# Fused attention stage of a two-layer decoder: opening reordered, output projection by quarters, convolution one frame ahead

## The chip, the cores and the metric

The kernel runs on one core of one Trainium2 chip. The metric is the device time of one launch in microseconds (us). One execution was profiled as well; every duration of a single instruction below comes from that one execution.

The engines are named as in the profile: PE is TensorE's matmul side and PEld its weight loads, DVE is VectorE, ACT is ScalarE, POOL is GpSimd, SP is SyncE, which only issues DMAs. Each of them works through a queue of its own in order, and they meet through semaphores.

## The reference

A decoder of two layers works on x (4 sequences, called frames here, of 512 positions and 256 channels) and a context of 4 x 512 x 192. The change concerns the first two of its six sublayers, which the kernel fuses into one stage. Cut to what matters:

```python
def _L0_attn_ref(x, ...):            # x is the layer-normed input; 16 heads of 32
    xc = causal_conv_4_taps(x, conv_w) + conv_b
    qk = einsum('btc,ec->bte', xc, qk_w).reshape(B, T, 16, 32)
    q = k = qk / max(norm(qk), 1e-12)
    v = einsum('btc,ec->bte', xc, v_w)
    g = sigmoid(einsum('btc,ec->bte', xc, g_w) + g_b)
    angles = t * freqs
    state = (v * cos(angles) + v * shift_by_one(k)) * g
    decay = gamma ** t
    mem = cumsum(state * decay, axis=1) / (decay + 1e-06)
    out = einsum('bte,ce->btc', mem * q, o_w)
    return layernorm(out) * ln_g + ln_b

x = x + _L0_attn_ref(layernorm(x), ...)
x = x + cross_attention(layernorm(x), ctx, Wq, bq, Wk, bk, Wv, bv, Wo, bo)   # 16 heads of 16, 512 x 512 softmax
```

The other four sublayers (a mixture of experts, and a second layer) come after the stage and are not touched.

## The kernel before, in words

`l0_mixers` holds the stage, one Python function with many small helpers, and has three parts. An **opening** loads weights and computes what the first frame needs before its first score. A **loop of 16 units** then runs the cross attention: a unit is four heads of one frame, so four units make a frame. A unit has eight score tiles of 128 x 1024 (`exponents`, L908 to L919): PE writes the scores into one of two PSUM pairs, DVE takes the row maxima (`tops`, L916), ACT takes the exponentials (`e`, L919); the sums over values follow a unit later (`gather_values`, L948). A short **tail** closes the last frame.

The first sublayer of a later frame runs inside the units of earlier ones. In the unit loop `after(n, f, ...)` puts a step f behind the n-th score tile of the unit, n from 0 to 7, its slot. With b the frame of the unit and m its number in the frame, `near_b` is b + 1 and `next_b` is b + 2. The steps of a frame are, in order:

- `normalize` (L725) normalizes x (DVE) and adds ln_b to x on POOL. `mix` (L739 to L750) turns a half of the channels on PE, copies it twice on ACT and does three taps of the convolution on DVE; there are two mixes for a frame.
- `measure` (L752) makes qk on PE for four heads' worth of channels and squares it on ACT; `total` (L767) sums the squares on PE; `scale`, `scale_near`, `scale_far` and `factor` (L772 to L797) send the sums through DRAM, take the inverse root on DVE (the rn chain), multiply by the decays, and spread the two factors over the channels by DMA.
- `gated_values` (L799) makes g and v, `recall` (L809 to L823) the running memory: a product with the factor on DVE, an add of cos on POOL, a product, a scan and two products on DVE. It ends in qk times memory (L823), in place.
- `emit` (L825 to L829) is the output projection: 32 passes on PE for a frame, four groups of channels summed into each of four row blocks, which fill two PSUM banks. It runs by halves: `emit(b, 0)` and `emit(b, 2)` each need all four groups, thus all four recalls. `absorb` (L831 to L840) is the layernorm of the result (its statistics are `ln_st` L179, in a helper) and the addition to x. `tokens`, `turn_tokens`, `split` and `keep` then make the queries of the cross attention.
- `keys` and `keep_keys` (L1018, L1023) make keys and values of a frame from the context, with a high and a low half of the keys (`low_k` is DVE's, L855), and put them in DRAM. All four frames' keys are made in the opening.

Only in the opening: `decays` (L675 to L692) doubles the powers of gamma in ten steps on DVE and stores them (`far_dec`); `cosines` (L703 to L719) needs `time`, an iota on POOL (L705), six DVE operations for each of four channel groups to reduce the angle, sine and square on ACT, and two operations on POOL, the last of which multiplies by a decay that `decay_of` (L698) loads by DMA. `fetch_bias` (L619 to L626) brings the key and query biases in eight loads each of 16 x 2 elements, in an order of its own, and v_bias comes in four loads; `dense` (L628) packs and scales weights and biases on POOL.

Two things set the order. Matmuls (`pinned`, L577) and loads on SP (`move`, L586) keep the order of the program; where one of them waits, what stands behind it on its engine waits too. All else is put in order ahead of time by the framework's scheduler, by its own estimates; each engine then executes its queue as it stands. Buffers are rotating pools: `bank` is four PSUM banks for all that isn't a score, `scratch` eight tiles of 128 x 516, `wide` (tag `e`) eleven tiles of 128 x 1024, `factors` two. The order of the opening is written out in L1034 to L1108, the slots in L1109 to L1187.

Of the kernel before, what the change touches and what calls it, by code (L numbers as in the profile page):

```python
# [19 lines left out]
NB = 4  # L20
# [520 lines left out]
def l0_mixers(k):  # L541
# [20 lines left out]
    with ExitStack() as es:  # L562
# [56 lines left out]
        def fetch_bias(n):  # L619
            bias[n] = wp.tile([P, 2], F32, name=f"b_{n}")  # L620
            for odd in range(2):
                for i in range(4):
                    at = 32 * (2 * (i % 2) + odd)
                    move(
                        bias[n][64 * odd + i : 64 * odd + 64 : 4, :], a[f"b{n}"][at : at + 16, i // 2 :: 2]
                    )  # L626
# [12 lines left out]
        conv_w, conv_b, qk_w = load("conv_w"), load("conv_b"), load_rows("qk_wT")  # L639

        gamma = wp.tile([16, 1], F32, name="gamma_sb")
        for r in range(4):
            move(gamma[4 * r : 4 * r + 4, :], a["gamma"][r::4, :])
        freqs, g_b, ln_b = load("freqs"), load("g_b"), load_all("ln_b")
        context(0)
        fetch("k", 96)
        w_v = wide("w_v")[:96, :, :256]
        move(w_v, a["Wv"].rearrange("(c p) f -> p c f", p=96))
        fetch_bias("k")
        v_w, g_w = load_rows("v_wT"), load_rows("g_wT")  # L650
        tc.keep_in_program_order(k.load_x(1))
# [19 lines left out]
        power = wp.tile([16, 10], F32, name="power")  # L671
        far_dec = dram.tile([2, 16, T], F32, name="far_dec", bufs=1)
        near_dec = wp.tile([P, 2, 64], F32, name="near_dec")

        def decays():  # L675

            dec = scratch("dec", T + 1)[:16]
            nc.vector.memset(dec[:, 0:1], 1.0)
            nc.vector.tensor_copy(power[:, 0:1], gamma)
            for j in range(9):  # L680
                n = 1 << j
                nc.vector.tensor_scalar_mul(dec[:, n : 2 * n], dec[:, 0:n], power[:, j : j + 1])
                nc.vector.tensor_mul(power[:, j + 1 : j + 2], power[:, j : j + 1], power[:, j : j + 1])
            nc.vector.tensor_copy(dec[:, T : T + 1], power[:, 9:10])
            for j in range(2):
                move(far_dec[j], dec[:, j : j + T])
            for j in range(2):
# [9 lines left out]

        def decay_of(m):  # L698
            decay = wk.tile([P, 2, T], F32, tag="factors", name=f"decay_{m}")[:, 0, :]
            by_channel(decay, lambda r: far_dec[0, 4 * r + m])  # L700
            return decay

        def cosines():  # L703
# [4 lines left out]
            for m in range(4):  # L708
# [6 lines left out]
                decay = decay_of(m)  # L715
# [3 lines left out]
                nc.gpsimd.tensor_mul(cos[:, m, :], ang, decay)  # L719
# [105 lines left out]
        def emit(b, i2):  # L825
            ps = outs[b, i2] = bank(f"o_{b}_{i2}").rearrange("p (i d) -> p i d", d=D)
            for i in range(2):
                at = (i2 + i) * P
                pinned(ps[:, i, :], [(raw[b][:, m, at : at + P], o_w[:, m, :]) for m in range(4)])  # L829

        def absorb(b):  # L831
            y = k.h_pool.tile([P, QT, D], F32, tag="h", name=f"y_{b}")
            srcs = [outs[b, i2][:, i, :] for i2 in (0, 2) for i in range(2)]
# [200 lines left out]
        normalize(0)  # L1034
        for c in range(DC):
            mix(0, c)
        decays()
        measures(0)
        cosines()
        nc.vector.memset(v_bias, 0.0)  # L1040
        nc.vector.tensor_scalar_mul(half_b, g_b, 0.5)
        dense("k", 96)
        scale(0)
        context(1)
        scale_near(0)
        o_w, ln_g = load_rows("o_wT"), load_all("ln_g")
# [3 lines left out]
        keys(0)  # L1050
        keep_keys(0)
        for m in range(4):
            gated_values(0, m)
        fetch("q", P)
        w_o = load_rows("Wo")
        recall(0, 0)
        factor(0, 2)
        recall(0, 1)
        factor(0, 3)
        b_o = load_all("bo")  # L1060
        fetch_bias("q")
        for r in range(4):
            move(v_bias[32 * r : 32 * r + 16, :], a["bv"].rearrange("o (m r d) -> r d (o m)", r=4, d=16)[r])
        normalize(1)
        for c in range(DC):
            mix(1, c)
        recall(0, 2)
        recall(0, 3)
        dense("q", P)
        for t in (*weighed, zeros):  # L1070
            nc.gpsimd.memset(t, 0.0)
        for i2 in (0, 2):
            emit(0, i2)
        context(2)
        tc.keep_in_program_order(k.load_x(2))
        absorb(0)
        keys(1)
# [7 lines left out]
        measures(1)  # L1085
        keep_keys(1)
        context(3)
        tc.keep_in_program_order(k.load_x(3))
        scale(1)
# [6 lines left out]
        gather(0)  # L1096
        fetch_values(0)
        scale_near(1)
        keys(2)
        scale_far(1)  # L1100
        for m in range(4):
            gated_values(1, m)
        for m in range(2):
            factor(1, m)
        recall(1, 0)
        keep_keys(2)
        keys(3)
        keep_keys(3)  # L1108
        units = 4 * NB  # L1109
        for u in range(units + 1):  # L1110
# [17 lines left out]
            near_b, next_b = b + 1, b + 2  # L1128
            if m == 0:
                if near_b < NB:  # L1130
# [5 lines left out]
                    after(7, emit, near_b, 0)  # L1136
                if next_b < NB:
                    after(6, normalize, next_b)
            elif m == 1:
# [5 lines left out]
                if near_b < NB:  # L1145
                    after(0, emit, near_b, 2)
                    after(1, absorb, near_b)
                    after(4, tokens, near_b)
                if next_b < NB:
                    for c in range(DC):  # L1150
                        after(1 + c, mix, next_b, c)
                    for j in range(4):
                        after(4 + j, measure, next_b, j)
                    for j in range(2):
                        after(6 + j, total, next_b, j)
            elif m == 2:
# [6 lines left out]
                if next_b < NB:  # L1163
                    for j in range(2):
                        after(j, total, next_b, 2 + j)
                    after(2, scale, next_b)
                    after(4, scale_near, next_b)
                    after(6, scale_far, next_b)
# [870 lines left out]
```

## Time and profile before

| | |
|---|---|
| median of 3 runs | 1348.41 us (1347.64 to 1352.46) |
| the profiled execution's own time | 1347.23 us |
| its span, first to last instruction | 1345.5 us, mean granted TensorE clock 0.842 |
| busy in the span | PE 1009.1, DVE 822.3, ACT 399.4, POOL 206.0 us |
| opening, until the first score matmul | 0 to 147.9 us |
| units of frame 0 | 147.9 to 254.8 us |
| units of frame 1 | 254.8 to 364.7 us |
| units of frame 2 | 364.7 to 467.2 us |
| units of frame 3 and the tail | 467.2 to about 552 us |
| the other sublayers | about 552 to 1345 us |

The profile is read so. A timeline row gives start and duration of an instruction or a run of equal ones, engine, line, operation, its output and inputs by the program's names, shape and count; a bracket at the end gives the time for which the engine had been idle and what it waited for. "PE L581 o<-o_wT_sb,qk" is a pass of the output projection. "SPq" is SP's queue, and a long duration there is a wait. A row of the table by stretch gives the stretch's length, then busy time and number of instructions for PE, PEld, DVE, ACT and POOL, then the granted TensorE clock (1.00 is full speed), the DMA engines' busy share, and GB/s. A waits row gives the engine, the waiting instruction, what it waited for, the sum in us, how many times, and the longest.

### The profile page before, as it was taken

How to read it: one execution, taken by the hardware profiler on the slowest of the kernel's cores; microseconds unless marked ns; L12 is line 12 of the kernel's file. 1: busy time of each engine (PE TensorE's matmuls, PEld its weight loads, DVE VectorE, ACT ScalarE, POOL GpSimd, SP SyncE). 2: the span in 40 equal slices, each digit the busy share in tenths (PEclk: the TensorE clock that was granted, in tenths of full speed). 3: DMA queues.
4: the chain of work that ended last, by engine and by line, in shares of the span. 5: the costliest groups of instructions: out<-in, count | busy, mean ns of one | idle time of the engine just before them, and what ended most of it. 6: DMA issues, size and time to landing. Idle time of an engine off the chain costs nothing. (4 is left out here: it accounts for less than half of the span.)

```text
span 1345.5 us, 11829 instructions
## 1 busy us (share of the span) xinstructions
PE 1009.1 (75%) x3734; PEld 551.9 (41%) x3734; DVE 822.3 (61%) x1989; ACT 399.4 (30%) x676; POOL 206.0 (15%) x224
## 2 busy tenths in 40 slices
PE   4759669669766768383589999849873787769997
PEld 1334333233332313163466677735442444245443
DVE  7665678787768766154256922254666555886564
ACT  2403426445534564100011421002311344730000
POOL 2421102202113011117000000351112110000000
PEclk9969769779976877766699999979876898979999
DMA  4445803624523220146466262551000010001000
GB/s 131 135 120 191 267 7 105 182 95 136 152 88 114 90 79 31 35 149 232 137 233 181 90 228 90 168 195 40 0 0 4 16 47 32 0 27 37 16 31 19
DMA packets 92344, 132.27 MB, mean 98 GB/s; under 512 B 21312, under 2 KB 62784, under 8 KB 92256
## 3 DMA queue, kind: packets, MB, share of 16 engines
q1 hardware_dynamic: 86768, 113.58, 27.0%
q0 software_dynamic: 5504, 17.83, 3.7%
q8 instruction: 32, 0.52, 0.2%
q14 instruction: 40, 0.33, 0.1%
HBM read 88.72 MB, written 42.66 MB: 98 GB/s over the span
## 5 line engine op out<-in xcount | busy, mean ns | idle before, releaser
L919 ACT ACTIVATE e<-score,tops 128x512 f32<-128x512 f32 x256 | 161.5, 686 | 164.3 <-DVE tops L916 93.0
L916 DVE TENSOR_REDUCE tops<-score 128x2 f32<-128x1024 f32 x128 | 155.6, 1220 | 51.3 <-PE score L581 51.0
L212 PE MATMUL y<-folded_sb,fht 128*128 128x512 f32 x256 | 112.7, 601 | 0.0
L954 PE MATMUL av<-e,weighed 128*32 128x512 f32 x512 | 88.7, 765 | 26.6 <-POOL weighed L942 26.6
L581 PE MATMUL score<-query,key 64*128 64x512 f32 x256 | 75.5, 588 | 36.7 <-ACT e L919 35.0
L1895 DVE SCALAR_TENSOR_TENSOR x_sb<-y,tt_w,x_sb 128x256 f32<-128x256 f32 x128 | 61.9, 483 | 38.3 <-PE y L212 35.0
L581 PEld LDWEIGHTS score<-query,key 64*128 64x128 f32 x256 | 27.8, 214 | 131.7 <-ACT e L919 69.1
L212 PE MATMUL ef<-sw,eact 128*128 128x256 f32 x320 | 79.4, 388 | 1.6 <-DVE ey L1413 1.6
L581 PE MATMUL o<-o_wT_sb,qk 128*128 128x256 f32 x128 | 43.2, 494 | 43.8 <-DVE qk L823 31.9
L212 PE MATMUL ef<-eht,sw 128*128 128x320 f32 x256 | 75.1, 437 | 0.6 <-ACT eact L1402 0.6
L212 PEld LDWEIGHTS y<-folded_sb,fht 128*128 128x128 f32 x256 | 48.9, 193 | 59.9 <-issue 59.9
L212 PE MATMUL fold<-w_out,w_in 128*128 128x256 f32 x256 | 66.6, 418 | 5.2 <-issue 5.2
L212 PEld LDWEIGHTS ef<-sw,eact 128*128 128x128 f32 x320 | 58.9, 194 | 12.4 <-DVE ey L1413 4.9
L212 PEld LDWEIGHTS fold<-w_out,w_in 128*128 128x128 f32 x256 | 53.1, 213 | 13.3 <-issue 5.5
L212 PEld LDWEIGHTS ef<-eht,sw 128*128 128x128 f32 x256 | 47.7, 190 | 18.4 <-ACT eact L1402 1.6
L581 PEld LDWEIGHTS o<-o_wT_sb,qk 128*128 128x128 f32 x128 | 29.8, 246 | 55.8 <-DVE qk L823 37.0
L212 PE MATMUL f<-aht,W_fT_sb 128*128 128x512 f32 x96 | 49.7, 668 | 1.4 <-DVE x_sb L1521 1.4
L1402 ACT ACTIVATE eact<-ef 128x640 f32<-128x640 f32 x32 | 22.4, 704 | 95.3 <-PE ef L212 95.2
L581 PE MATMUL xo<-Wo_sb,att 128*128 128x256 f32 x128 | 37.1, 439 | 17.1 <-POOL att L995 17.1
L1437 POOL DMA_INDIRECT got<-table,rows x32 | 31.0, 970 | 105.3 <-DMA table<-ey 94.0
L942 POOL TENSOR_TENSOR weighed<-v,weighed 128x256 f32<-128x256 f32 x16 | 10.6, 663 | 229.9 <-ACT weighed L941 229.9
L203 PE MATMUL turn<-ident,h 128*128 128x128 f32 x96 | 19.1, 342 | 34.5 <-DVE h L190 33.8
(370 smaller groups left out, 1794.5 us busy)
## 6 DMA issues: line engine op xcount, KB each, us to landing
table<-zeros POOLq DMA_DIRECT2D x8, 1152.0 KB, 6.9
factors<-far SPq DMA_DIRECT2D x64, 128.0 KB, 6.2
key<-far_k SPq DMA_DIRECT2D x16, 512.0 KB, 4.1
query<-far_q SPq DMA_DIRECT2D x16, 512.0 KB, 5.8
w_in<-in_w_in SPq DMA_DIRECT2D x8, 1024.0 KB, 6.5
w_out<-in_w_outT SPq DMA_DIRECT2D x8, 1024.0 KB, 12.6
rows<-table SPq DMA_DIRECT2D x8, 640.0 KB, 5.1
table<-ey SPq DMA_DIRECT2D x8, 640.0 KB, 4.8
```

Of the source, the lines that this page charges most:

```text
L203: nc.tensor.transpose(ps[:, i * P : (i + 1) * P], h[:, i, c * P : (c + 1) * P], self.ident)
L212: self.nc.tensor.matmul(out, lhs_t, rhs, start=(i == 0), stop=(i == len(pairs) - 1))
L581: nc.tensor.matmul(out, lhs_t, rhs, start=start and i == 0, stop=stop and i == len(pairs) - 1)
L916: nc.vector.tensor_reduce(top, ps, AX.X, ALU.max, negate=True)
L919: nc.scalar.activation(e[:, i, :], ps[:, i, :], AF.Exp, bias=top[:, i : i + 1])
L942: weighing[0] = nc.gpsimd.tensor_mul(wt[:, :, :, 0:16], vs[u], wt[:, :, :, 16:17].to_broadcast([P, QT, 4, 16]),)
L954: nc.tensor.matmul(avs[u][32 * h : 32 * h + 32, :], weighed[u % 2][:, j, h, :], es_of[u, h // 2, j][:, h % 2, :], start=(j == 0), stop=(j ...
L1402: nc.scalar.activation(act[:, f, :].rearrange("p (j t) -> p j t", j=2), ps[:, :, :half], AF.Silu)
L1437: nc.gpsimd.indirect_dma_start(out=got, out_offset=None, in_=k.table, in_offset=bass.IndirectOffsetOnAxis(ap=k.rows[:, which, t : t + 1], ...
L1895: nc.vector.scalar_tensor_tensor(xt, ps[:, e, :], w[:, i, e4 + e : e4 + e + 1], xt, ALU.mult, ALU.add)
```

## The change

It has four parts, all in `l0_mixers`.

First, who issues loads: b_k, b_q (8 loads each) and v_bias (4) are issued by POOL instead of SP, and gamma comes in one load on ACT's queue instead of four on SP's.

Second, the opening: the doubling of the decays runs on ACT; the 16 decay loads follow at once into two tiles of the pool `wide`, and the loads of the context, Wk, Wv and of frame 1's x stand behind them; `near_decays` is split off. `scale(0)` stands directly behind `measures(0)`, `gated_values(0)` ahead of `keys(0)`, frame 1's mixes ahead of the first recall, `keys(1)` and `keys(2)` between the recalls, `keys(3)` ahead of `turn_tokens(0)`, and frame 2's normalize and mixes at the end of the opening. On POOL's queue, as the scheduler orders it, all 20 loads, the scaling of both biases and three memsets stand ahead of `time`.

Third, the output: `emit(b, m)` takes one group of channels, 8 passes, into all four row blocks. Both banks are opened by a matmul of zeros (`nought`, one row of bfloat16), so that all 32 passes accumulate. In the loop the quarters stand in slots 1, 3 and 5 of a frame's first unit and slot 0 of its second.

Fourth, the loop: normalize and mix of a frame run three frames ahead (`last_b`), in slot 5 of the third unit and slots 5 and 6 of the fourth; in the loop that is frame 3 alone. measure, total, scale, scale_near and scale_far start one or two slots earlier, and the first recall moves from slot 6 to slot 4.

```diff
@@ -621,7 +621,7 @@
                     at = 32 * (2 * (i % 2) + odd)
-                    move(
+                    nc.gpsimd.dma_start(
                         bias[n][64 * odd + i : 64 * odd + 64 : 4, :], a[f"b{n}"][at : at + 16, i // 2 :: 2]
@@ -636,19 +636,12 @@
             nc.gpsimd.tensor_scalar_mul(bias[n], bias[n], scales[n])
+        gamma = wp.tile([16, 1], F32, name="gamma_sb")
+        nc.scalar.dma_start(gamma, a["gamma"].rearrange("(m r) o -> r m o", r=4))
         conv_w, conv_b, qk_w = load("conv_w"), load("conv_b"), load_rows("qk_wT")
-        gamma = wp.tile([16, 1], F32, name="gamma_sb")
-        for r in range(4):
-            move(gamma[4 * r : 4 * r + 4, :], a["gamma"][r::4, :])
         freqs, g_b, ln_b = load("freqs"), load("g_b"), load_all("ln_b")
-        context(0)
-        fetch("k", 96)
-        w_v = wide("w_v")[:96, :, :256]
-        move(w_v, a["Wv"].rearrange("(c p) f -> p c f", p=96))
-        fetch_bias("k")
         v_w, g_w = load_rows("v_wT"), load_rows("g_wT")
-        tc.keep_in_program_order(k.load_x(1))
         v_bias = wp.tile([P, 4], F32, name="v_bias")
@@ -669,21 +662,30 @@
         power = wp.tile([16, 10], F32, name="power")
+        decay_of = []
+        nought = wp.tile([1, P], BF16, name="nought")
         far_dec = dram.tile([2, 16, T], F32, name="far_dec", bufs=1)
...
             dec = scratch("dec", T + 1)[:16]
-            nc.vector.memset(dec[:, 0:1], 1.0)
-            nc.vector.tensor_copy(power[:, 0:1], gamma)
+            nc.gpsimd.memset(dec[:, 0:1], 1.0)
+            nc.scalar.copy(power[:, 0:1], gamma)
             for j in range(9):
                 n = 1 << j
-                nc.vector.tensor_scalar_mul(dec[:, n : 2 * n], dec[:, 0:n], power[:, j : j + 1])
-                nc.vector.tensor_mul(power[:, j + 1 : j + 2], power[:, j : j + 1], power[:, j : j + 1])
-            nc.vector.tensor_copy(dec[:, T : T + 1], power[:, 9:10])
+                nc.scalar.activation(dec[:, n : 2 * n], dec[:, 0:n], AF.Copy, scale=power[:, j : j + 1])
+                nc.scalar.activation(power[:, j + 1 : j + 2], power[:, j : j + 1], AF.Square)
+            nc.scalar.copy(dec[:, T : T + 1], power[:, 9:10])
             for j in range(2):
                 move(far_dec[j], dec[:, j : j + T])
+            for m2 in range(2):
+                decay = wide(f"decay_{m2}")
+                for m in range(2):
+                    by_channel(decay[:, m, :], lambda r: far_dec[0, 4 * r + 2 * m2 + m])
+                decay_of.extend(decay[:, m, :] for m in range(2))
+        def near_decays():
             for j in range(2):
@@ -694,11 +696,6 @@
         cos = wp.tile([P, 4, T], F32, name="cos")
-        def decay_of(m):
-            decay = wk.tile([P, 2, T], F32, tag="factors", name=f"decay_{m}")[:, 0, :]
-            by_channel(decay, lambda r: far_dec[0, 4 * r + m])
-            return decay
         def cosines():
@@ -712,11 +709,10 @@
                     nc.vector.scalar_tensor_tensor(ang, turns, -piece, ang, ALU.mult, ALU.add)
-                decay = decay_of(m)
                 nc.scalar.activation(ang, ang, AF.Sin, scale=0.5)
...
                 nc.gpsimd.tensor_scalar(ang, ang, -2.0, 1.0, ALU.mult, ALU.add)
-                nc.gpsimd.tensor_mul(cos[:, m, :], ang, decay)
+                nc.gpsimd.tensor_mul(cos[:, m, :], ang, decay_of[m])
         normal, mixed, raw, sums_of, squares, factors, gated, outs = {}, {}, {}, {}, {}, {}, {}, {}
@@ -822,15 +818,20 @@
             nc.vector.tensor_mul(qk, mem, qk)
-        def emit(b, i2):
-            ps = outs[b, i2] = bank(f"o_{b}_{i2}").rearrange("p (i d) -> p i d", d=D)
-            for i in range(2):
-                at = (i2 + i) * P
-                pinned(ps[:, i, :], [(raw[b][:, m, at : at + P], o_w[:, m, :]) for m in range(4)])
+        def emit(b, m):
+            if m == 0:
+                outs[b] = [bank(f"o_{b}_{i2}").rearrange("p (i d) -> p i d", d=D) for i2 in range(2)]
+                for out in outs[b]:
+                    pinned(out, [(nought, nought[:, None, :].to_broadcast([1, 4, P]))], True, False)
+            for i in range(QT):
+                lhs_t, rhs = raw[b][:, m, i * P : (i + 1) * P], o_w[:, m, :]
+                pinned(outs[b][i // 2][:, i % 2, :], [(lhs_t, rhs)], False, m == 3 and i % 2 == 1)
         def absorb(b):
             y = k.h_pool.tile([P, QT, D], F32, tag="h", name=f"y_{b}")
-            srcs = [outs[b, i2][:, i, :] for i2 in (0, 2) for i in range(2)]
+            srcs = [outs[b][i // 2][:, i % 2, :] for i in range(QT)]
             mv = k.moments(srcs, sp)
@@ -1032,49 +1033,67 @@
         normalize(0)
+        decays()
+        context(0)
+        fetch("k", 96)
+        w_v = wide("w_v")[:96, :, :256]
+        move(w_v, a["Wv"].rearrange("(c p) f -> p c f", p=96))
         for c in range(DC):
             mix(0, c)
-        decays()
+        tc.keep_in_program_order(k.load_x(1))
+        near_decays()
         measures(0)
+        scale(0)
+        nc.vector.memset(v_bias, 0.0)
+        nc.vector.memset(nought, 0.0)
+        nc.vector.tensor_scalar_mul(half_b, g_b, 0.5)
+        fetch_bias("k")
+        dense("k", 96)
+        o_w, ln_g = load_rows("o_wT"), load_all("ln_g")
+        scale_near(0)
         cosines()
-        nc.vector.memset(v_bias, 0.0)
-        nc.vector.tensor_scalar_mul(half_b, g_b, 0.5)
-        dense("k", 96)
-        scale(0)
+        for m in range(4):
+            gated_values(0, m)
+        normalize(1)
         context(1)
-        scale_near(0)
-        o_w, ln_g = load_rows("o_wT"), load_all("ln_g")
         scale_far(0)
...
         keys(0)
+        for c in range(DC):
+            mix(1, c)
+        fetch_bias("q")
+        for r in range(4):
+            nc.gpsimd.dma_start(
+                v_bias[32 * r : 32 * r + 16, :], a["bv"].rearrange("o (m r d) -> r d (o m)", r=4, d=16)[r]
+            )
+        recall(0, 0)
+        factor(0, 2)
         keep_keys(0)
-        for m in range(4):
-            gated_values(0, m)
+        keys(1)
         fetch("q", P)
         w_o = load_rows("Wo")
-        recall(0, 0)
-        factor(0, 2)
+        b_o = load_all("bo")
+        emit(0, 0)
         recall(0, 1)
         factor(0, 3)
-        b_o = load_all("bo")
-        fetch_bias("q")
-        for r in range(4):
-            move(v_bias[32 * r : 32 * r + 16, :], a["bv"].rearrange("o (m r d) -> r d (o m)", r=4, d=16)[r])
-        normalize(1)
-        for c in range(DC):
-            mix(1, c)
+        context(2)
+        tc.keep_in_program_order(k.load_x(2))
+        keep_keys(1)
+        emit(0, 1)
+        keys(2)
         recall(0, 2)
+        dense("q", P)
+        emit(0, 2)
         recall(0, 3)
-        dense("q", P)
         for t in (*weighed, zeros):
             nc.gpsimd.memset(t, 0.0)
-        for i2 in (0, 2):
-            emit(0, i2)
-        context(2)
-        tc.keep_in_program_order(k.load_x(2))
+        emit(0, 3)
+        context(3)
+        keep_keys(2)
         absorb(0)
-        keys(1)
+        measures(1)
+        scale(1)
         v_wide = scratch("v_wide").rearrange("p (m c) -> p m c", c=P)
@@ -1082,11 +1101,7 @@
         tokens(0)
-        measures(1)
-        keep_keys(1)
-        context(3)
-        tc.keep_in_program_order(k.load_x(3))
-        scale(1)
+        keys(3)
         for c in range(DC):
@@ -1094,18 +1109,19 @@
         gather(0)
+        scale_near(1)
+        scale_far(1)
         fetch_values(0)
-        scale_near(1)
-        keys(2)
-        scale_far(1)
+        for m in range(2):
+            factor(1, m)
+        tc.keep_in_program_order(k.load_x(3))
+        keep_keys(3)
         for m in range(4):
             gated_values(1, m)
-        for m in range(2):
-            factor(1, m)
         recall(1, 0)
-        keep_keys(2)
-        keys(3)
-        keep_keys(3)
+        normalize(2)
+        for c in range(DC):
+            mix(2, c)
         units = 4 * NB
@@ -1125,7 +1141,7 @@
                 after(3, blank, u - 2)
-            near_b, next_b = b + 1, b + 2
+            near_b, next_b, last_b = b + 1, b + 2, b + 3
             if m == 0:
@@ -1133,9 +1149,8 @@
                     after(5, recall, near_b, 3)
-                    after(7, emit, near_b, 0)
-                if next_b < NB:
-                    after(6, normalize, next_b)
+                    for j in range(3):
+                        after(1 + 2 * j, emit, near_b, j)
             elif m == 1:
@@ -1143,16 +1158,14 @@
                 if near_b < NB:
-                    after(0, emit, near_b, 2)
+                    after(0, emit, near_b, 3)
                     after(1, absorb, near_b)
...
                 if next_b < NB:
-                    for c in range(DC):
-                        after(1 + c, mix, next_b, c)
                     for j in range(4):
-                        after(4 + j, measure, next_b, j)
-                    for j in range(2):
-                        after(6 + j, total, next_b, j)
+                        after(2 + j, measure, next_b, j)
+                    for j in range(4):
+                        after(4 + j, total, next_b, j)
             elif m == 2:
@@ -1161,11 +1174,11 @@
                 if next_b < NB:
-                    for j in range(2):
-                        after(j, total, next_b, 2 + j)
-                    after(2, scale, next_b)
-                    after(4, scale_near, next_b)
-                    after(6, scale_far, next_b)
+                    after(0, scale, next_b)
+                    after(2, scale_near, next_b)
+                    after(4, scale_far, next_b)
+                if last_b < NB:
+                    after(5, normalize, last_b)
                 if 1 <= b:
@@ -1174,7 +1187,10 @@
                 after(3, factor, next_b, 1)
-                after(6, recall, next_b, 0)
+                after(4, recall, next_b, 0)
+                if last_b < NB:
+                    for c in range(DC):
+                        after(5 + c, mix, last_b, c)
             if u:
```

## Prediction

> **What bounds the kernel now.** I read the page first (spans by engine, then the 40 slices), then the windows of the fused attention stage unit by unit, then the waits of VectorE and SyncE inside it, then the timelines. The change touches the first 552 us only; the remaining 793 us run the same code, so I cost them at nothing. The table by stretch gives, for each, the sum over PE, weight loads, VectorE, ScalarE and GpSimd, then clock, DMA share and GB/s:
>
> ```profile
> 147.90:180.00 32.10, 12.72 (x35) 6.75 (x34) 21.93 (x27) 10.62 (x17) 5.25 (x5) 0.57 0.60 184
> 180.00:210.90 30.90, 26.43 (x97) 9.79 (x97) 27.50 (x85) 15.64 (x28) 3.68 (x5) 0.83 0.08 24
> ...
> 254.80:286.10 31.30, 18.16 (x69) 7.50 (x69) 22.62 (x31) 12.01 (x20) 5.94 (x7) 0.62 0.48 144
> 286.10:316.90 30.80, 26.33 (x96) 9.77 (x96) 26.64 (x72) 16.36 (x29) 8.46 (x10) 0.83 0.29 95
> ...
> 467.20:484.30 17.10, 11.52 (x53) 3.23 (x53) 10.43 (x12) 10.72 (x18) 0.64 (x1) 0.70 0.19 69
> ```
>
> The last row is a unit with nothing but its own attention: 17.1 us. Units 0, 1, 4, 5 carry the side work of later frames and take 31 to 32. In units 1 and 5 VectorE is busy 26.6 to 27.5 us of 31; in units 0 and 4 neither engine is full. What is lost there shows in VectorE's waits between 180 and 210.9 us, and in PE's timeline around it:
>
> ```profile
> DVE ln_st L179 <- PE o L581: 5.7, 2, 4.5
> ...
> 175.60 4.42 PE L581 MATMUL o<-o_wT_sb,qk 128*128 128x256 f32 x10 [3.94 <-DVE qk L823]
> 179.95 0.50 PE L581 MATMUL score<-query,key 64*128 64x512 f32 x2
> 180.38 3.72 PE L581 MATMUL o<-o_wT_sb,qk 128*128 128x256 f32 x16
> 184.03 0.50 PE L581 MATMUL score<-query,key 64*128 64x512 f32 x2
> ```
>
> PE stands idle 3.94 us for the last qk, then does 26 of the 32 out-projection passes in one heap, with the score pairs at 179.95 and 184.03 queued behind them; VectorE, done with its queue at 175.5, waits 4.5 us. The same heap recurs at 282.0 and 389.97 (VectorE waits 4.2 and 4.7).
>
> The opening ends with the first score at 147.91. From about 100 us PE never rests (47.8 of 50 us), but before that it is busy 56 of 100. SyncE's and GpSimd's timelines:
>
> ```profile
> 22.90 22.74 SPq L588 DMA_DIRECT2D decay<-far_dec  x16
> 45.74 0.36 SPq L588 DMA_DIRECT2D far_ss<-sums  x1
> ...
> 16.32 0.60 POOL L705 IOTA time<- 128x512 f32 x1
> ...
> L1007 POOL DMA_DIRECT2D table<-zeros x8: 1022/1022/1317, 219.5 to 405.2; - x8
> ```
>
> SyncE holds far_ss until 45.74, though sums are ready at 38: ahead of it are 16 decay loads that wait for two buffers, which cos on GpSimd frees (longest wait 15.3 us).
>
> **The change, part by part.**
>
> *Output by quarters.* Of the heap of 26 passes (4.42 + 3.72 = 8.1 us) the last quarter alone, 8 passes, stays behind the last recall. Earlier quarters, 24 passes, fall into slots 1, 3 and 5 of units 0, 4 and 8, where PE has 12 to 19 us free: nothing, as long as scores stay ahead of VectorE. Without that cover they would cost 24 x 0.44 = 10.6. Here a rule weighs. The heap's first ten passes took 0.44 us each, its last sixteen 0.23, so it warmed itself. The Trainium skill, "TensorE: Matmul & The Clock Gate", Part 1, says that the array halves its clock after an idle window of about 3.4 us and needs a busy one to regain it; it adds that ramps are under 1% of a typical kernel. By its aside the last quarter is 8 x 0.23 = 1.9; by the row (clock 0.50 from 165 to 175) 3.5, and unit 1 then starts cold, at most half of one window, 1.8, lost. I take 3.5: the heap shrinks by 4.6, about VectorE's 4.2 to 4.7 wait. The score pair that stood behind it comes forward too, worth up to the 3.9 of idle ahead of the heap. So a frame gains from 2.8 (4.6 - 1.8) to 8.5 (4.6 + 3.9).
>
> *Two zero matmuls open each frame's banks.* No bf16 row with one weight row exists; the nearest, 128x512, has a pitch of 0.43 warm and 0.86 cold. Bounds 0 and 1.7 us a frame; PE idles there, so 0. The two banks are held, though, from slot 1 until absorb has read them, half of the four banks. qk of the next frame needs them and scores are queued behind qk on PE, so a late absorb (about 5 us of VectorE) stops scores. Bounds 0 to 5 a frame; I take 1, since qk comes at slot 2, one tile behind absorb.
>
> *Convolution a frame ahead.* A mix is six VectorE passes, 4.3 to 4.4 us, plus 8 turns on PE. Frame 2's goes from unit 1 to the opening's end (its VectorE work lies in unit 0, as the queue orders show), frame 3's from unit 5 to unit 3. Unit 5 becomes 30.8 - 4.4 - about 1 of heap = 25.5, where PE's 26.3 less the moved passes binds. Unit 3 has 19.4 of VectorE in 26.3, so it takes the mix for 1.7. Unit 0 has 21.9 of 32.1 but in a chain of recalls: I add 2 to 3.
>
> By frames, before to after: frame 0, 32.1 + 30.9 + 17.6 + 26.3 = 107 to 34.5 + 26 + 17.6 + 28 = 106, -1. Frame 1, 110 to 25.5 + 25.5 + 21.5 + 25.4 = 98, -12: unit 4 loses the heap before its last boundary (3.9 + part of 4.1), unit 5 the wait and the mix. Frame 2, 102.5 to 25 + 27 + 26 + 17 = 95, -7.5. Frame 3 has none of it. Less about 1 for the banks: **-19.5**; bounds -26 (8.5 in three frames) and -8 (2.8 in three).
>
> *Opening, biases from GpSimd.* 20 tiny loads go from SyncE (8 x 0.71, 8 x 0.63, 4 x 0.50 = 12.7 us of issue) to GpSimd, into its queue ahead of the iota `time`; behind that stand VectorE's angles, then the rn chain, recalls, everything. The row: a GpSimd load takes 1.02 us, so 20.4, and with scalings and memsets iota starts near 36 rather than 16.3. The rn chain then ends near 62 instead of 54.87. The Trainium skill, "DMA: Bandwidth & Descriptors", sends simple loads to Sync (Issuing engine by pattern), which speaks against; yet its Anatomy section puts 0.05 us on dispatch, little on descriptors, and most of a fixed 2.0 on completion. With that, GpSimd is free early, rn ends near 52 and the first score comes ten sooner. I go by the row, with the pitch of GpSimd's indirect loads (1.28) as the dear end: rn near 67.
>
> *Opening, decays on ScalarE, loads unblocked.* ScalarE idles until 11.85, so its 19 small operations (0.23 each, 4.5) replace six us of VectorE; the convolution begins near 13.5 instead of 17.2. Decay loads go into free buffers: far_ss leaves near 32. That 14 us gain is swallowed: rn now waits for VectorE, which waits for iota. Two more table loads (1.28 each) fall into PE's idle time.
>
> *Opening from rn's end (R) on.* Before: absorb ends at R + 46.8, tokens turn at R + 60.5, first score R + 93.0. After: -5.0 for the output heap (7.7 to 2.7), +3.0 for four low_k (0.75) between recalls, +8 for a new stall: ctx(2) is behind a factors load on SyncE that waits for recall 1, and low_k of frame 2 is ahead of recall 2 on VectorE; -2.1 for factors that land unseen. Absorb ends R + 50.7. To the turn 15.0 instead of 13.7: keys(3), 7 us, replaces measures, which move beside absorb. From turn to score 20.7 instead of 32.5, since keys(2) and keys(3), 6.9 each, are gone (2 comes back as q's round trip). First score at R + 86.4. So 138, **148**, 153 for R of 52, 62, 67, against 147.9: 0 likeliest, between -10 and +5. gamma's one load on ScalarE's queue (1.4 us of SyncE before) is inside the 13.5.
>
> Sum: the profiled execution took 1347.2 (span 1345.5); less 19.5 it is 1327.7. It lies 1.2 below the median of the runs, 1348.4, so I say 1329.
>
> **Rivals.**
>
> *Cheap GpSimd loads.* The opening gains 10 as well: 1348.4 - 29.5 = 1319, and 1312 with the loop's best. For it: the page above, and tiny loads (16 by 2 elements against 1152 KB). Against: 1022 was least and median of the eight and indirect ones take 970, so it looks fixed. 0.20.
>
> *Loop gain given back.* Scores wait behind qk for a bank until absorb, and PE stays cold: 2.8 a frame, 8 in all, gives 1340; with dear loads 1345. For it: VectorE is busy 27 us of units 1 and 9, so a wait removed only shows the next. Against: units 1 and 5 have full-clock PE. 0.22.
>
> *Slower: GpSimd's loads hold iota.* One mechanism: at p us per load the first score is 20 x (p - 1.02) late. If the page's whole 2.0 us were paid in turn, 19.6 late; with the loop's 8 that is 1360. It decides (over 6.7 slower) from p = 1.77 with the small loop gain, 2.3 with the likely one. Against: nothing on GpSimd's queue here has such a pitch. 0.08.
>
> The likeliest, as summed, has 0.50 (own range 1322 to 1336). The range from 1312 to 1346 leaves out the slower case and the outermost of the two others.
>
> A measurement of this kernel can tell about 0.5%, 6.7 us, from no change. Faster by more than that (under 1341.7): all of the likeliest and the cheap case and four tenths of the third, 0.79; within: 0.15; slower: 0.06.
>
> **What would show each step.** First score near 148, with GpSimd's iota near 36 and load pitch 1.0; SyncE's wait for cos gone and far_ss near 32; VectorE's waits "ln_st from o" under 1.5 us in units 1, 5 and 9; only 8 o passes between the last recall and absorb, at 0.44; unit 5 near 25, unit 4 near 26, unit 3 longer by 2. I am wrong if iota starts by 22 (then the opening gains), if units 1, 5, 9 keep a wait for o or show score behind qk, or if the tail after 552 changes length.

## The result, and the profile after

The changed kernel took 1339.81 us (median of 16 runs, 1329.77 to 1346.67) against 1347.59 for the kernel before in 16 runs beside it; the ratio is 0.9945, 95% interval 0.9923 to 0.9967. That is 7.4 us less, between 4.4 and 10.4. Forecast was 1329, 19.5 less: the direction was right, the gain is about two fifths of what was forecast.

From here on a unit is bounded by VectorE's first row maximum in it (`tops`, eight to a unit, 128 in every trace). Several expectations take the changed kernel's bounds from its scores, a tile too late: their 42.7 and 30 for units 0 and 4 are 38.3 and 26.1 by row maxima, e5's 18.6 and 4.7 are 20 and 6. In us:

| | forecast change | before | after | measured change |
|---|---|---|---|---|
| opening, to the first row maximum | 0 | 148.4 | 145.4 | -3.0 |
| frame 0 (units 0 to 3) | -1 | 107.2 | 113.2 | +6.0 |
| frame 1 | -12 | 109.9 | 101.8 | -8.1 |
| frame 2 | -7.5 | 102.1 | 96.4 | -5.7 |
| end of frame 2 | -19.5 with the banks | 467.7 | 456.8 | -10.9 |

The profiled span fell by 7.2 (1345.5 to 1338.3), not 10.9: the rest, the same code in both, took 877.8 before and 881.5 after. Over all kernels of this study it took 874 to 886 in a single profile, so I compare stages by these bounds and whole times by the ratio to runs of the kernel before on the same chip. Each kernel has one profile: a stage's figure is one execution's, a ratio that of several.

The table by stretch of the changed kernel shows units 0, 1, 4 and 5, the columns as before:

```profile
145.40:183.70 38.30, 15.20 (x42) 9.18 (x40) 28.54 (x37) 11.46 (x19) 6.91 (x7) 0.67 0.59 176
183.70:209.80 26.10, 24.09 (x87) 9.13 (x87) 23.67 (x77) 14.77 (x27) 3.40 (x5) 0.90 0.09 28
258.60:284.70 26.10, 16.70 (x76) 8.04 (x76) 22.48 (x30) 10.16 (x18) 6.11 (x7) 0.76 0.34 101
284.70:311.90 27.20, 24.38 (x84) 8.89 (x85) 23.16 (x66) 14.70 (x27) 6.37 (x8) 0.88 0.33 108
```

Units 1 and 4 are near the forecast's 26 and 25.5; unit 5, forecast at 25.5, is 1.7 us longer. Unit 0 is far off: 38.3 against 34.5, and VectorE is idle for a quarter of it. Of VectorE's waits, the first block is unit 1, the second unit 0:

```profile
DVE ln_st L179 <- PE o L581: 1.8, 2, 0.9
```

```profile
DVE tops L917 <- PE score L581: 4.8, 3, 3.5
...
DVE term L811 <- DMA factors<-far: 0.7, 1, 0.7
```

The wait for o in unit 1 fell from 5.7 to 1.8, as planned. In unit 0 a wait of row maxima for scores has come, and one for factors. PE's and VectorE's timelines at the start of unit 0 show both:

```profile
144.82 0.73 PE L581 MATMUL score<-query,key 64*128 64x512 f32 x4
145.49 0.60 PE L581 MATMUL o<-nought 1*128 1x512 bf16 x2
153.71 3.78 PE L581 MATMUL o<-o_wT_sb,qk 128*128 128x256 f32 x8 [7.63 <-DVE qk L819]
157.42 1.07 PE L581 MATMUL score<-query,key 64*128 64x512 f32 x4
```

```profile
145.37 2.36 DVE L917 TENSOR_REDUCE tops<-score 128x2 f32<-128x1024 f32 x2 [0.55 <-PE score L581]
148.41 0.69 DVE L811 TENSOR_TENSOR term<-qk,factors 128x512 f32<-128x512 f32 x1 [0.69 <-DMA factors<-far]
```

The recall of frame 1's first group (call it recall 1,0) begins at 148.41, three us after the first row maximum, and ends at 153.66; the first quarter waits 7.63 us for it with the next score pairs behind it. Before, recall 1,0 began at 141.81, 6.6 ahead of the first row maximum:

```profile
141.81 0.69 DVE L815 TENSOR_TENSOR term<-qk,factors 128x512 f32<-128x512 f32 x1
...
148.45 2.35 DVE L916 TENSOR_REDUCE tops<-score 128x2 f32<-128x1024 f32 x2
```

SyncE's timeline in the changed kernel tells why it is late:

```profile
116.75 0.34 SPq L588 DMA_DIRECT2D far_ss<-sums  x1
126.01 0.36 SPq L588 DMA_DIRECT2D far_v<-v  x1
...
133.71 0.58 SPq L588 DMA_DIRECT2D rn<-far_ss  x1
141.66 1.20 SPq L588 DMA_DIRECT2D far<-rn  x2
...
144.19 3.58 SPq L588 DMA_DIRECT2D factors<-far  x8
```

Frame 1's sums are stored at 116.75, but their reload for rn goes out at 133.71, behind the values of frame 3 (126.01) and the queries; keys(3), now ahead of the queries on PE, holds both. Frame 1's factors go out at 144.19; before, 135.52.

The opening's other steps, from SyncE's and GpSimd's timelines:

```profile
16.62 7.27 SPq L588 DMA_DIRECT2D decay<-far_dec  x16
...
31.39 0.33 SPq L588 DMA_DIRECT2D far_ss<-sums  x1
...
13.63 2.99 POOL L624 DMA_DIRECT2D b_k<-in_bk  x6
...
24.29 0.59 POOL L702 IOTA time<- 128x512 f32 x1
```

The decay loads run through (22.7 us before), far_ss leaves at 31.39 instead of 45.74, both as forecast. GpSimd's tiny loads take 0.50 us each (six in 2.99), half of what I took from the 1152 KB store.

### The profile page after: what moved, and what is told of

Same layout as the page of the kernel before. It is cut to its first block, busy times and chain, and to the rows that moved or that the text cites. A ratio compares the mean times of both kernels' runs of the same rounds, so it can differ in the third digit from the quotient of the medians.

```text
span 1338.3 us, 11843 instructions
## 1 busy us (share of the span) xinstructions
PE 1015.5 (76%) x3742; PEld 559.0 (42%) x3742; DVE 812.9 (61%) x1969; ACT 405.0 (30%) x698; POOL 213.9 (16%) x245
## 3 DMA queue, kind: packets, MB, share of 16 engines
q1 hardware_dynamic: 85648, 113.58, 27.2%
## 5 line engine op out<-in xcount | busy, mean ns | idle before, releaser
L212 PE MATMUL y<-folded_sb,fht 128*128 128x512 f32 x256 | 113.0, 601 | 0.0
L955 PE MATMUL av<-e,weighed 128*32 128x512 f32 x512 | 84.2, 700 | 19.7 <-POOL weighed L943 19.7
L212 PE MATMUL fold<-w_out,w_in 128*128 128x256 f32 x256 | 69.0, 423 | 14.2 <-issue 14.2
L581 PEld LDWEIGHTS score<-query,key 64*128 64x128 f32 x256 | 27.2, 212 | 123.4 <-ACT e L920 71.8
L581 PE MATMUL o<-o_wT_sb,qk 128*128 128x256 f32 x128 | 51.0, 567 | 34.6 <-DVE qk L819 34.6
L212 PEld LDWEIGHTS fold<-w_out,w_in 128*128 128x128 f32 x256 | 53.8, 216 | 22.7 <-issue 15.0
L581 PEld LDWEIGHTS o<-o_wT_sb,qk 128*128 128x128 f32 x128 | 35.0, 287 | 49.7 <-DVE qk L819 40.0
L1418 ACT ACTIVATE eact<-ef 128x640 f32<-128x640 f32 x32 | 22.4, 702 | 96.4 <-PE ef L212 96.3
L1453 POOL DMA_INDIRECT got<-table,rows x32 | 31.1, 972 | 104.6 <-DMA table<-ey 94.2
L1398 PE MATMUL eturn<-ident,rows 128*128 128x128 f32 x80 | 16.9, 295 | 34.6 <-DMA rows<-table 30.8
```

Source lines behind the costliest of these rows:

```text
L212: self.nc.tensor.matmul(out, lhs_t, rhs, start=(i == 0), stop=(i == len(pairs) - 1))
L581: nc.tensor.matmul(out, lhs_t, rhs, start=start and i == 0, stop=stop and i == len(pairs) - 1)
L955: nc.tensor.matmul(avs[u][32 * h : 32 * h + 32, :], weighed[u % 2][:, j, h, :], es_of[u, h // 2, j][:, h % 2, :], start=(j == 0), stop=(j ...
L1398: nc.tensor.transpose(ps[:, c, :], rows[:, i, c * P : (c + 1) * P], k.ident)
L1418: nc.scalar.activation(act[:, f, :].rearrange("p (j t) -> p j t", j=2), ps[:, :, :half], AF.Silu)
L1453: nc.gpsimd.indirect_dma_start(out=got, out_offset=None, in_=k.table, in_offset=bass.IndirectOffsetOnAxis(ap=k.rows[:, which, t : t + 1], ...
```

## The experiments

Two theories came first. A: each quarter stands on PE ahead of scores, so the first unit of a frame is held by its place. B: the convolution moved into the first units lengthens them. Each kernel was timed beside the kernel before; "end of frame 2" is the first row maximum of unit 12.

**e1_halves.** `emit` as before (both halves after the last recall, in opening and loop) in the changed kernel:

```diff
-                    for j in range(3):
-                        after(1 + 2 * j, emit, near_b, j)
+                    after(7, emit, near_b, 0)
...
-                    after(0, emit, near_b, 3)
+                    after(0, emit, near_b, 2)
```

> The changed kernel with its output projection by halves again, as before (both halves behind the last recall); everything else new. Theory A (each quarter stands on PE in front of score pairs and waits for its recall, so the first unit of a frame is held): unit 0 falls from 42.7 to about 36 us, units 4 and 8 from 30 to about 28, while units 1, 5, 9 get VectorE's wait for o back, 4 us each; the whole within 5 us of the changed kernel. Theory B (the convolution moved into the first units is what lengthens them): unit 0 stays above 40 and the waits of 4 to 5 us in units 1, 5, 9 come on top, so about 12 us slower than the changed kernel.

Ratio 1.0072 (1.0048 to 1.0097). Opening 151.0, frames 113.9, 112.3 and 99.7, end of frame 2 476.9; unit 0 38.9. Without quarters unit 0 is as long, so their place does not make it so: against A. The total, 17 us slower than the changed kernel, is nearer B's. The quarters are worth 1.3% here.

**e2_mix_back.** The loop's convolution, measure, scale and first recall in their slots of before:

```diff
-        normalize(2)
-        for c in range(DC):
-            mix(2, c)
...
+                    for c in range(DC):
+                        after(1 + c, mix, next_b, c)
```

> The changed kernel with normalize, mix, measure, total, scale and the first recall of a later frame in their slots of before; the quarters and the opening stay new. Theory A: unit 0 loses only the 4.3 us of convolution (about 38), units 4 and 8 stay near 30, units 1 and 5 get 4 us longer; 3 to 6 us slower than the changed kernel. Theory B: unit 0 falls to about 33 and unit 4 to 26, units 1 and 5 grow by 4; 4 to 8 us faster than the changed kernel.

Ratio 0.9994 (0.9979 to 1.0009). Unit 0 38.1, unit 1 31.1 (26.1 in the changed kernel), unit 5 32.2; end of frame 2 462.9. Unit 0 stays long without the convolution: against B. The 0.5 points (6.6 us) by which it is slower than the changed kernel are what the convolution ahead is worth there.

**e3_late_quarters.**

```diff
-                    for j in range(3):
-                        after(1 + 2 * j, emit, near_b, j)
+                    for j, slot in enumerate((3, 5, 7)):
+                        after(slot, emit, near_b, j)
```

> The changed kernel with the first three quarters of the output in slots 3, 5 and 7 of a frame's first unit instead of 1, 3 and 5. Theory A: when a quarter comes its recall is done, so unit 0 falls from 42.7 to about 37, units 4 and 8 from 30 to 27; 8 to 12 us faster than the changed kernel. Theory B: units 0, 4 and 8 as they are, the whole within 3 us.

Ratio 0.9956 (0.9939 to 0.9974); unit 0 36.7, frame 0 113.0, end of frame 2 458.3. A falls here too: the recalls end when they did (153.8, 163.8, 176.2 and 183.7; 153.7, 163.7, 175.8 and 183.8 in the changed kernel), so later quarters free nothing. The profile is of the fastest of its eleven runs.

**e4_time_first.**

```diff
+        time = scratch("time")
+        tc.keep_in_program_order(nc.gpsimd.iota(time, ...))
         normalize(0)
...
-                    nc.gpsimd.dma_start(
+                    tc.keep_in_program_order(nc.gpsimd.dma_start(
```

> The changed kernel with the iota time ahead of the bias loads on GpSimd's queue, at 9 us instead of 24. As the prediction had it (the loads hold the iota, and all behind it): VectorE's wait for time, 6.7 us, goes and the first score comes 6 us sooner, at about 139. Rival: the angles then meet another wait (the decays on ScalarE, the tables) and the first score moves by less than 2 us.

Ratio 0.9901 (0.9884 to 0.9917); first score at 141.05 instead of 144.82, end of frame 2 453.2. The edit keeps GpSimd's bias loads in program order as well. The result lies between the two forecasts: 3.8 of the 6.7 us of waiting come through; in the place of the iota VectorE's angles now wait 3.7 us for the sums on PE.

Next I took the change apart, by its two ends and the quarters alone.

**e5_opening_only.** e1's and e2's edits together, so that only the opening is new:

```diff
-        emit(0, 3)
+        for i2 in (0, 2):
+            emit(0, i2)
...
+                    for c in range(DC):
+                        after(1 + c, mix, next_b, c)
```

> The changed kernel with halves and with the convolution in its old slots: of the change only the opening is left. If the parts add (undoing the quarters moved the end of frame 2 by 18.6 us, undoing the convolution ahead by 4.7), frame 2 ends near 481 us against 467 before: the new opening alone makes the kernel some 14 us slower, by what it leaves to frame 0. Rival: the parts depend on each other, and the opening alone gives what its first score shows, 3 to 5 us faster than before, frame 2 ending near 463.

Ratio 1.0063 (1.0042 to 1.0085): the opening alone makes the kernel 8.5 us slower. First row maximum 149.9 (148.4 before), frames 112.5, 109.3, 101.3, end of frame 2 473.0 (467.7 before), between the two forecasts: the parts do not add. Frame 0 alone is 5.3 longer. Recall 1,0 ends 12.8 us after the first row maximum.

**e6_loop_only.** The old opening with the new loop; the opening's quarters all stand at emit's old place:

```diff
-        for i2 in (0, 2):
-            emit(0, i2)
+        for j in range(4):
+            emit(0, j)
...
+        normalize(2)
+        for c in range(DC):
+            mix(2, c)
         units = 4 * NB
```

> The kernel before, its opening untouched but for frame 2's normalize and mix at its end, with the new loop: quarters and convolution ahead. If the parts add, frame 2 ends near 444 us, 23 us faster than before and faster than the changed kernel. Rival: the loop is worth only what the changed kernel's loop shows (309.4 us of units against 319.3), so frame 2 ends near 460, 7 us faster than before.

Ratio 0.985 (0.9815 to 0.9885), 20 us faster than before. First row maximum 145.4, frames 108.1, 98.9 and 96.1, end of frame 2 448.5, nearer the 444 of added parts than the 460. At the same first row maximum as the changed kernel, unit 0 is 4.7 us shorter. Its line by stretch, and its recall 1,0, which ends ahead of the first row maximum:

```profile
145.40:179.00 33.60, 14.23 (x42) 8.20 (x40) 25.48 (x32) 11.44 (x19) 5.18 (x5) 0.66 0.56 167
```

```profile
137.90 0.69 DVE L816 TENSOR_TENSOR term<-qk,factors 128x512 f32<-128x512 f32 x1
...
142.98 0.68 DVE L824 TENSOR_TENSOR qk<-mem,qk 128x512 f32<-128x512 f32 x1
...
145.43 2.36 DVE L922 TENSOR_REDUCE tops<-score 128x2 f32<-128x1024 f32 x2 [0.90 <-PE score L581]
```

**e6b_quarters_only.** e6 without the convolution ahead:

```diff
-        normalize(2)
-        for c in range(DC):
-            mix(2, c)
...
+                    for c in range(DC):
+                        after(1 + c, mix, next_b, c)
```

> The kernel before with the quarters in the loop and nothing else. The forecast had it worth the waits of 4.2 to 4.7 us in three frames, 13 us. Theory A (quarters hold the scores of the first unit behind the recalls, cold): unit 0 grows by 5 to 8 us, units 4 and 8 by 2 or shrink little, and what is left is 5 us or less.

Ratio 0.9905 (0.9878 to 0.9931). First row maximum 141.4: in the opening the quarters give 7.0. Frames 107.7, 107.7, 98.8: in the loop only 5.1. Unit 0 did not grow (31.1). VectorE's wait for o in unit 1 fell to 1.8 and yet the unit took 32.1: VectorE and PE are busy for 28.3 and 27.6 us of it. So A's small gain came, but not for A's reason:

```profile
172.50:204.60 32.10, 27.64 (x95) 10.37 (x95) 28.32 (x89) 18.41 (x33) 3.69 (x5) 0.77 0.14 46
```

**e7_warm.** Twelve passes of zeros ahead of each of unit 0's first three quarters:

```diff
+            if b == 1 and m < 3:
+                for _ in range(12):
+                    pinned(outs[b][0], [(nought, nought[:, None, :].to_broadcast([1, 4, P]))], False, False)
```

> The changed kernel with twelve more passes of zeros on PE ahead of each of the three quarters in unit 0, where PE waits 5 to 8 us for the recall; they add zeros to the opened bank. If the half clock is what lengthens unit 0, the three quarters fall from 3.78 to about 1.9 us each and unit 0 from 42.7 to about 37. If only the place of the quarters ahead of the scores matters, unit 0 stays within 2 us of 42.7, or grows.

Ratio 0.9934 (0.9908 to 0.9961), unit 0 39.6. The trial did not warm the quarters: a row of zeros took 0.23 us, the twelve 2.76, PE then idled again, and the quarter behind them still ran at half clock (0.50 from 164.76 to 168.54):

```profile
159.22 2.76 PE L581 MATMUL o<-nought 1*128 1x512 bf16 x12
164.76 3.78 PE L581 MATMUL o<-o_wT_sb,qk 128*128 128x256 f32 x8 [2.79 <-DVE qk L819]
```

Whether warm quarters would shorten unit 0 stays open.

A and B had fallen, and e5 and e6 put the loss into the new opening. That it ends 3.0 us sooner in the changed kernel is the quarters' doing: without them (e5) it ends no sooner than the old one. Theory C: the opening hands frame 1 over later, with recall 1,0 still to do. D: key stores crowd unit 0's loads.

**e9_keys3_late.**

```diff
         tokens(0)
-        keys(3)
...
-        keep_keys(3)
         for m in range(4):
             gated_values(1, m)
+        keys(3)
+        keep_keys(3)
```

> The changed kernel with frame 3's keys and their loads moved back behind the gated values of frame 1, so that the queries and frame 1's rn come about 7 us sooner on PE and SyncE while PE's total before the first score is the same. Theory C (the new opening reaches the first score with frame 1's factors not landed, so that a fourth recall falls into unit 0): first row maximum near 146, unit 0 from 38.3 to about 33, frame 2 ends near 451 instead of 456.8; 5 to 7 us faster than the changed kernel. Theory D (unit 0 is long because 2 MB of key stores crowd its loads): they still come at 148 us or later, so unit 0 stays at 38.

Ratio 0.9908 (0.9871 to 0.9946), 5.0 us better than the changed kernel's, though the intervals overlap. First row maximum 145.5, recall 1,0 at 142.11 instead of 148.41, unit 0 34.5, frame 0 109.2: C holds. The key stores still go out from 145.17 on, so D does not. Frames 1 and 2 were 2.1 and 1.8 longer in its profile, so frame 2 ended at 456.8, not at 451.

**e10_rn_early.**

```diff
         scale(1)
+        scale_near(1)
+        scale_far(1)
+        for m in range(2):
+            factor(1, m)
...
-        scale_near(1)
-        scale_far(1)
         fetch_values(0)
```

> The changed kernel with only the loads of frame 1's rn and factors issued on SyncE directly behind frame 1's sums instead of behind frame 0's queries; PE's order stays. Theory C: recall 1,0 is done about when the first score comes, unit 0 falls from 38.3 to about 33, frame 2 ends near 451. Rival: what holds recall 1,0 is not the load but its place on VectorE's queue behind the gated values, and unit 0 moves by less than 2.

Ratio 0.99 (0.9858 to 0.9942). SyncE now sends the reload and frame 1's factors early:

```profile
119.37 0.36 SPq L588 DMA_DIRECT2D rn<-far_ss  x1
127.11 1.20 SPq L588 DMA_DIRECT2D far<-rn  x2
129.65 3.57 SPq L588 DMA_DIRECT2D factors<-far  x8
```

Recall 1,0 ran from 142.87 to 149.64, the first row maximum came behind it at 150.2, and unit 0 took 28.0. Part of that is the later start; but unit 1, too, began 5.5 us sooner (178.2 for 183.7), and opening and frame 0 together ended at 252.4 against 258.6, even ahead of e6's 253.5. Frame 2 ended at 453.1; 451 was expected. The ratio's interval overlaps the changed kernel's: in whole time this gain is not clear of noise.

**e11_rn_time.** e10 and e4 together.

```diff
+        time = scratch("time")
+        tc.keep_in_program_order(nc.gpsimd.iota(time, ...))
...
         scale(1)
+        scale_near(1)
+        scale_far(1)
```

> The same as the last, and the iota time ahead of GpSimd's loads. If the two gains add (5 to 6 us from the loads, 3.6 from the iota), frame 2 ends near 447 and the kernel is 9 us faster than the changed one, the best so far with the new opening; if the opening is held by something else once rn is early, it is within 2 us of the last kernel.

Ratio 0.9861 (0.982 to 0.9902); unit 0 27.6, end of frame 2 447.5. As far as the intervals show, the two add. Against e4, which has the same opening but for these loads, unit 1 begins 7.3 us sooner.

**e12_all_early.** e11 and e9 together.

```diff
         tokens(0)
-        keys(3)
...
+        keys(3)
+        keep_keys(3)
```

> The last kernel (frame 1's rn and factors loaded early, iota time first) with frame 3's keys behind the gated values as well, so that the queries too come 7 us sooner. Theory C: the first row maximum returns from 146 to about 142 with recall 1,0 done or nearly so, unit 0 stays near 28 to 31, frame 2 ends near 444; the fastest of all, 12 us or more below the changed kernel. If the early rn and the late keys cure the same thing, it is within 2 us of the last kernel.

Ratio 0.988 (0.9854 to 0.9905), first row maximum 149.7 where 142 was expected, unit 0 27.6, end of frame 2 447.5. The late keys add nothing to the early rn. e6, e11 and e12 beat both kernels and can't be told apart by these intervals.

Over the traces, unit 0 goes with the place of recall 1,0:

| | end of recall 1,0 after the first row maximum | unit 0 | unit 1 begins |
|---|---|---|---|
| before | -0.9 | 32.3 | 180.7 |
| e6 | -1.8 | 33.6 | 179.0 |
| e9 | +3.1 | 34.5 | 180.0 |
| changed | +8.3 | 38.3 | 183.7 |
| e10 | -0.6 | 28.0 | 178.2 |
| e4 | +8.9 | 39.3 | 180.9 |
| e11 | -0.6 | 27.6 | 173.6 |

e1, e2, e3, e5 and e7 (+9.0 to +12.8) have 36.7 to 39.6.

## Why the prediction missed the size

**The step that failed** is the one headed "Opening from rn's end (R) on", which closed with "0 likeliest, between -10 and +5". It took the first score for the end of the opening, and priced only what leads to that score, not what had to be done beside it: it moved keys(3) ahead of the queries and did not follow SyncE's queue, where frame 1's reload stands behind the values of frame 3 and the queries. Recall 1,0, 5.2 us from its first instruction to its last, slid past the first score, and the first quarter with it. That is unit 0's 38.3 where 34.5 was forecast, and most of frame 0's +6.0 where -1 was. For the 0, the runs show a loss: e5 prices the new opening at +0.63% alone (8.5 us), and the changed kernel is 0.95 points (about 13 us; the intervals allow 5 to 20) slower than e6, which has the new loop without it. Moving SyncE's loads of frame 1 and nothing else takes unit 0's excess away, twice (e10 against the changed kernel, e11 against e4); e9, which moves the keys on PE and VectorE too, takes most of it.

By stage the changed kernel ends frame 2 8.3 us after e6: 5.2 of it in frame 0, which e10 gets back, and 2.9 in frame 1. The latter is the granted clock, not the opening. Unit 5 of e6:

```profile
279.60:303.90 24.30, 21.20 (x84) 7.39 (x85) 22.59 (x67) 14.71 (x27) 6.40 (x8) 1.00 0.43 121
```

The same 84 passes take PE 24.38 us at 0.88 in the changed kernel, and the unit 27.2. Of the eight kernels with this loop, e6, e7 and e11 had 1.00 there and 24.3 us, the others 0.87 to 0.93 and 25.9 to 27.2. e7 has the new opening, so that is not what decides; what does is not shown.

**The first score** came about where the sum put it (144.8; 148 forecast), by luck: two errors cancel. GpSimd's loads took 0.50 us for 1.02, so iota came at 24.29 for 36 and rn ended at 53.6 for 62; had R alone been wrong, R + 86.4 would have given 140. The stall on ctx(2) took it back; 8 was forecast for what VectorE's waits give as 15.0:

```profile
DVE low_k L856 <- ACT high_k L855: 15.0, 2, 12.8
```

So the rival of cheap loads had its premise right and its gain wrong. The slower rival was wrong at its root. e4 shows that the iota still costs 3.8.

**The loop** was near as a sum: with the old opening its frames gave +0.8, -11.0 and -6.0, 16.2 against 19.5 forecast, and three more came in the opening. Its split was wrong. I credited the quarters with 2.8 to 8.5 us a frame. Alone they give 5.1 in all three frames (e6b), under the lowest of that, for with the wait gone unit 1 is still filled by VectorE's convolution. With the old opening the convolution ahead then gave 11.1 more (e6 less e6b). With the new opening the quarters alone gave 4.0 (e2 less e5), the convolution alone nothing (e1 less e5: 2.8 longer over three frames, ratios 1.0072 and 1.0063), and both 11.7. My rival "a wait removed only shows the next" describes each half taken alone; together they work. That rival was set aside because "units 1 and 5 have full-clock PE"; the rows shown have 0.83 there. And the forecast put frame 2's mixes at nothing for the opening: the first row maximum comes 4.0 later with them in the old one (e6, e6b), 1 to 2 in the new.

**The heap** left 8 passes, as said. They took 3.78 us ahead of frame 1's absorb, 3.60 ahead of frame 2's and 1.99 ahead of frame 3's. The forecast's 3.5, from the row, is right for two of them; its 1.9, by the aside of the Trainium skill, "TensorE: Matmul & The Clock Gate", Part 1, that ramps are small, for the third, and for frame 2's in e6, e7 and e11 (1.99).

**What stays open.** The four us between stage and span: PE idles 14.2 us ahead of `fold` passes with nothing recorded as its cause, 5.2 before, in code that is the same. By ratio the new opening may cost more than the 5.2 us of frame 0; where the rest would lie is not shown.

## What to carry to other kernels

An opening doesn't end with the first instruction of the loop. Before a reorder is called neutral, list everything that the loop's first stretch takes as done, and follow each item through every queue, the DMA queue above all; here it was a chain that is not on the way to the first score that slipped. And two changes that take load off the same stretch should be summed there together: each alone can be worth little where the other's load is the next bound.

## What the runs showed of the hardware

A load issued by GpSimd cost its queue 0.50 us for 16 x 2 elements and a store 1.02 us for 1152 KB, so the price is not fixed.

One-row bfloat16 passes of zeros did not keep PE's clock up. In e7 they filled 3.41 us at full clock together with the score passes ahead of them, and the next 3.41 us had half:

```profile
145.02:148.43 3.41, 3.41 (x19) 1.43 (x18) 2.49 (x3) 1.47 (x3) 0.00 (x0) 1.00 0.83 213
148.43:151.84 3.41, 1.04 (x3) 0.13 (x1) 1.39 (x2) 3.27 (x6) 1.54 (x1) 0.50 0.81 204
```

From 158.68 to 162.09 it was the same: PE busy for 3.30 us at 1.00, then half from there to 165.50. Ordinary passes of 2.52 us in as long a stretch kept the full clock (the changed kernel, 188.91 to 192.32).
